# A graph layer on one core: gathering two groups ahead from group 44, and a paired group's permutation behind the gather

## The chip, the core and the metric

The kernel runs on one core of a Trainium2 chip. A core has five engines with a queue of instructions each: PE (TensorE, matrix products), ACT (ScalarE), DVE (VectorE), POOL (GpSimd) and SP (SyncE, which only issues DMAs here). Each engine works through its own queue in order and waits where an instruction needs another engine's result. The metric is device time in microseconds (us).

## The reference

A message-passing layer over 12,500 nodes with 128 features and 400,000 edges, sorted by `dst`:

```python
h = relu(layernorm(x)) @ W_in2f.T
Wij = (smu(edge_attr_20 @ W_f1.T + b_f1) @ W_f2.T + b_f2) * edge_weight[:, None]
agg = segment_sum(h[dst] * Wij, src, 12500)
out = x + smu(agg @ W_o1.T + b_o1) @ W_o2.T + b_o2
```

`smu(x)` is a smooth bend of `x`, made with erf. What is gathered is `h[dst]`, and the sum goes by `src`, which is in no order.

## The kernel before

**Tiles and groups.** The 400,000 edges are 3125 tiles of 128. Four tiles are a group (782 groups), two groups a super. The loop `for p in range(len(seq))` handles one group per turn; `at(p)` is the group of turn `p`. The supers are cut into ten epochs (`PARTS`, 56 supers or 112 groups each at first). The words "first pass" below mean the first epoch, turns 0 to 111.

**What happens to a group.** Its way is spread over several turns of the loop:

- `load` (SP): edge attributes `f`, targets `rbc` and the window `hw` of 42 rows of `h`, for the super three ahead;
- `pick_part` (ACT, two activations, lines 578 and 579): the 0/1 matrix `oh` that picks a row of the window for each edge;
- `hide` (PE, line 779) and `bend` (ACT, line 787): the hidden layer of the edge network, through the PSUM bank `pu`;
- `bins`, `count`, `read`, `number` (DVE and PE): for each edge the bin of 128 source nodes that it belongs to, and its place `ix` in that bin's buffer in DRAM;
- `gather` (PE, line 815): the product of `oh` and `hw` into the bank `ph`, which is `h[dst]`;
- `take` (ACT, line 834, four per group): that product times the edge weight, copied to `hg`;
- `weigh` (PE, lines 859 and 860): the edge network's output into the bank `pw`;
- `mix` (DVE, line 889): `pw` times `hg` into the rows `ms`, with the place inside the bin in column 128 (ACT);
- `send`, `scatter` (POOL, line 959): one indirect DMA per tile writes the 128 rows to their places.

**The sums.** In an epoch the rows that the epoch before wrote are read back (`fetch`, `rw`), a 0/1 matrix `se` is made (`choose`, DVE line 1004), and PE adds up the rows of each bin (`add`, line 1017) into a bank `pg`; after four bins DVE adds the bank to `agg` (line 1030). `parts` issues these products in two portions per turn. Where `pu_names` has two names, `pg` is always the bank `pg0`, and `parts` returns early rather than begin a new block of four bins with few products to go.

**Paired groups.** 125 groups are paired: their four tiles go out with two wide scatters and one extra one, `lt`, which a later group, the host, sends. `spread_keys`, `match` (DVE), `rank_left` and `place_left` make three pairs of 0/1 matrices, `permute` (PE, line 746, twelve products) brings the second two tiles' rows (`cd`) into the order of the first two, into the bank `pt`. `take_pairs` then reads that bank: DVE makes `lat`, the left-over rows' bin and place (lines 756 and 757), and ACT copies the rows (lines 759 and 760). `bins` and `number` of the host use `lat`, four or more groups later. Accesses of two engines to one bank are kept apart in the order in which the program issues them, reads too.

**The node stage.** During the first pass `step()` issues, three times a turn, the next of the steps that normalise `x`, transpose it, multiply it with the input weights, split it into three parts and write it to `h_dram`, through the banks `pg0` and `pg1` in turn; the splitting of the edge attributes stands there too (`todo`).

**Order.** The queues of PE, DVE, ACT and SP follow the order in which the program issues. What the turn does about the change, before:

```python
if p <= AHEAD_FROM:
    gather(at(p + 1)); take(at(p + 1))
parts(lo + (hi - lo) // 2)
mix(at(p + 1))
if g in paired:
    permute(g); take_pairs(g); send(g)
if at(p + 1) in paired:
    match(at(p + 1))
if p >= AHEAD_FROM:
    gather(at(p + 2)); take(at(p + 2))
```

(two calls to a line here). Behind it stand `hide` and `bend` for `p + 2`, or past `AHEAD_FROM` for `p + 3`, then `count(at(p + 2))`, `pick_part(at(p + 3))`, `bins(at(p + 3))`, `read(at(p + 2))`. `AHEAD_FROM` is 112, the first turn of the second pass; at that turn `pu_names` becomes `["pg1", "pu"]`, so that `hide` has two banks from there on.

Of the kernel before, what the change touches and what calls it, by code (L numbers as in the profile page):

```python
# [15 lines left out]
ALU = mybir.AluOpType  # L16
# [22 lines left out]
ROW = P + 1  # L39
# [3 lines left out]
NOBIN = 200.0  # L43
NOBIN_ROW = float(1 << 17)
# [3 lines left out]
def gnn_kernel(  # L48
# [19 lines left out]
    nc = tc.nc  # L68
# [14 lines left out]
    PER = SUP // GRP  # L83
    NG = (NT + GRP - 1) // GRP
    eps_of, left = [], NS
# [9 lines left out]
    for a, n in eps_of:  # L95
        paired = n if len(CAP) < len(eps_of) - SENT_LAST else 0
# [100 lines left out]
    drow = const.tile([P, EPOCHS], F32, name="drow")  # L197
# [124 lines left out]
    with tc.tile_pool(name="ld", bufs=4) as ld, \  # L322
# [24 lines left out]
        pu_names = ["pu"]  # L347
# [151 lines left out]
        def at(p):  # L499
            return seq[p] if p < len(seq) else NG  # L500
# [4 lines left out]
        epoch = [k for k, (a, n) in enumerate(eps_of) for _ in range(n)]  # L505
        first = {a * PER: k for k, (a, n) in enumerate(eps_of)}
        loaded, onehot, bins_of, slots, hidden, taken = {}, {}, {}, {}, {}, {}
        paired, host, wanting, since_pair = {}, {}, [], 0
# [75 lines left out]
        def s_of(g):  # L584
            return g // PER
# [143 lines left out]
        def place_left(g):  # L729
# [5 lines left out]
                                    irow_ps.unsqueeze(1).to_broadcast([P, 2, P]),  # L735
                                    at_.unsqueeze(2).to_broadcast([P, 2, P]), op=ALU.is_equal)

        def permute(g):

            pp, cd = matched.pop(g)[1], apart_of.pop(g)  # L740
            po = ps1.tile([P, GRP * P], F32, name="pt")
            for j in range(3):
                w = ROW + 2 if j == 2 else ROW
                for i in range(2):
                    o = (4 + i if j == 2 else 2 * i + j) * P
                    nc.tensor.matmul(po[:, j * (ROW + 2):j * (ROW + 2) + w], pp[:, o:o + P], cd[:, i, :w],  # L746
                                     start=(i == 0), stop=(i == 1))
            matched[g] = po

        def take_pairs(g):  # L750

            po, ms, k = matched.pop(g), mixed[g], epoch[s_of(g)]
            lt = cnt.tile([P, ROW], F32, name="lt", bufs=2)
            at_ = cnt.tile([P, 2], F32, name="lat")
            o = 2 * (ROW + 2)
            nc.vector.tensor_scalar(at_[:, 0:1], po[:, o + ROW:o + ROW + 1], NOBIN, None, op0=ALU.add)
            nc.vector.tensor_scalar(at_[:, 1:2], po[:, o + ROW + 1:o + ROW + 2], NOBIN_ROW, drow[:, k:k + 1],  # L757
                                    op0=ALU.add, op1=ALU.min)
            nc.scalar.activation(ms[:, 1::2, :], po[:, :o].rearrange("p (j r) -> p j r", j=2)[:, :, 0:ROW], AF.Copy)  # L759
            nc.scalar.activation(lt, po[:, o:o + ROW], AF.Copy)  # L760
            left_of[g] = (lt, at_[:, 0:1], at_[:, 1:2])
# [28 lines left out]
        def smooth(g):  # L790
            if g >= NG:
                return
            if new(g):
                units_of.pop(g)
                return
            n = groups[g][1] * P
            sm = edge.tile([P, GRP * P], F32, name="sm", bufs=3)
            nc.vector.scalar_tensor_tensor(sm[:, :n], units_of.pop(g)[:, :n], LIN, hidden[g][:, :n],
                                           op0=ALU.mult, op1=ALU.add)
            hidden[g] = sm  # L800
# [116 lines left out]
        def send(g):  # L917

            if by_edge(g):
                scatter(g, mixed.pop(g))  # L920
                return
            t, n = groups[g]
            ms = msg.tile([P, GRP, ROW], F32, name="ms")
            places_in(g, ms)
            pt = mixed.pop(g)
            for j in range(n):
                nc.scalar.activation(ms[:, j, 0:P], pt[:, j], AF.Copy, scale=w_sb[:, t + j:t + j + 1])
            if s_of(g) >= EARLY:
                nc.scalar.dma_start(kept_rows[:, t - kept_tile:t - kept_tile + n, :], ms[:, :n, :])
                return  # L930
            scatter(g, ms)
# [543 lines left out]
            todo.setdefault(10 + i, []).append(f)  # L1475

        k = 0
        SOON, SLACK, AHEAD_FROM = 10, 40, eps_of[1][0] * PER
        for p in range(len(seq)):
            g = seq[p]  # L1480
            s = g // PER
            if p == (FEW // SUP - 3) * PER:
                assert not opening
            if p % PER == 0:
                load(sup_at(p // PER + 3))
            if s < EARLY:
                k = chores(g)
            else:
                lo = hi = done
            if SOON < p < SLACK:  # L1490
                turn(at(p))
                send(at(p))
            if p >= SLACK:
                if by_edge(g) and g not in paired:
                    send(g)
                if p > SLACK and not by_edge(at(p - 1)):
                    turn(at(p - 1))
                    send(at(p - 1))
            for f in todo.pop(p, []):
                f()  # L1500
            if p > AHEAD_FROM:
                smooth(at(p + 2))
            step()
            number(at(p + 1))
            weigh(at(p + 1))
            if at(p + 1) in paired:
                spread_keys(at(p + 1))
            if p <= AHEAD_FROM:
                gather(at(p + 1))
                take(at(p + 1))  # L1510
            parts(lo + (hi - lo) // 2)
            mix(at(p + 1))
            if g in paired:
                permute(g)
                take_pairs(g)
                send(g)
            if at(p + 1) in paired:
                match(at(p + 1))
            if p >= AHEAD_FROM:
                gather(at(p + 2))  # L1520
                take(at(p + 2))
            if p == 0:
                turn(at(1))
                send(at(1))
            if p >= SOON:
                step()
            if p <= AHEAD_FROM:
                hide(at(p + 2))
                bend(at(p + 2))
            else:  # L1530
                hide(at(p + 3))
                bend(at(p + 3))
            if p < SOON:
                step()
            count(at(p + 2))
            if p <= AHEAD_FROM:
                smooth(at(p + 2))
            if 0 < p < SOON:
                turn(at(p + 1))
                send(at(p + 1))  # L1540
                if p == 1:
                    pick_part(at(3))
            if p == AHEAD_FROM:
                assert taken_steps == COUNT
                pu_names[:] = ["pg1", "pu"]
                hide(at(p + 3))
                bend(at(p + 3))
            pick_part(at(p + 3 - (p == 0)))
            bins(at(p + 3))
            if at(p + 1) in paired:  # L1550
                rank_left(at(p + 1))
            read(at(p + 2))
            if at(p + 1) in paired:
                place_left(at(p + 1))
            parts(hi)
            step()
            assert k == 0 or taken_steps == COUNT
# [291 lines left out]
```

## Time and profile before

| | us |
|---|---|
| median of three runs | 4024.81 (4022.95 to 4025.37) |
| profiled execution | 4014.04 |
| its span | 4012.3 |
| busy PE / DVE / ACT / POOL in the span | 3315.2 / 3264.7 / 2837.0 / 2949.5 |

The profile is one execution, told by the hardware profiler. Busy time counts an engine's instructions, not the DMAs that it issues nor the time it waits. A row of a group of instructions has the source line, the engine, the operation, what is written and read, the count, the busy time and the mean of one, and the idle time just before, with what ended it. A row of the list of waits has who waited, for whom, the total, the times and the longest. A row of the timeline has start, duration, engine, line, operation, operands, count and in brackets the idle time before.

### The profile page before, as it was taken

Reading aid. Unit: us, or ns where it says so; the run is one execution under the profiler, and the core shown is the slowest. Engines: PE = TensorE matmul, PEld = TensorE weight load, DVE = VectorE, ACT = ScalarE, POOL = GpSimd, SP = SyncE. Lnnn points to the kernel's source line nnn. Section 1 sums busy time; section 2 is a strip of 40 time slices with the busy share of each in tenths; the row PEclk is TensorE's granted clock in tenths of the full one; section 3 lists DMA queues with packets and bytes.
Section 4 is the critical chain, followed back from the end, with each engine's and each line's share of the span. In section 5 each row is a group of like instructions: output and inputs, shape, how many; then the busy total and the mean of one; then the engine's idle time right before and its main releaser. Section 6 shows DMA issues by size and latency. Waiting matters only on the chain.

```text
span 4012.3 us, 85549 instructions
## 1 busy us (share of the span) xinstructions
PE 3315.2 (83%) x25912; PEld 2821.8 (70%) x26245; DVE 3264.7 (81%) x8658; ACT 2837.0 (71%) x7473; POOL 2949.5 (74%) x3044
## 2 busy tenths in 40 slices
PE   7766776888888888888888888888988888798658
PEld 4345655777777777777777777777887777687548
DVE  7886667888888888888888888888998888897447
ACT  6757787777877777788788887777777777675002
POOL 6765657777777777777777777777777777777776
PEclk9878788999999999999999999999999999999889
DMA  5775767888987777887787778877888777786878
GB/s 165 228 220 165 210 185 232 256 254 248 267 248 227 225 211 216 229 240 214 211 230 229 220 230 235 231 220 225 237 238 235 210 204 221 211 244 203 269 239 252
DMA packets 659903, 906.21 MB, mean 226 GB/s; under 512 B 181396, under 2 KB 446488, under 8 KB 659306
## 3 DMA queue, kind: packets, MB, share of 16 engines
q1 hardware_dynamic: 552009, 673.07, 59.1%
q0 software_dynamic: 100112, 215.31, 16.6%
q10 hardware_dynamic: 7312, 12.29, 0.9%
q8 instruction: 208, 3.41, 0.4%
q14 instruction: 262, 2.14, 0.2%
HBM read 507.13 MB, written 393.21 MB: 224 GB/s over the span
## 4 chain that ended last, share of the span: by engine, by line
PE 24%; DVE 16%; DMA 16%; ACT 11%; issue 9%; POOL 8%; SPq 1%; DVEq 0%; ACTq 0%; POOLq 0%
DMA buf<-ms,ix 12%; PE pg L1017 8%; POOL buf L959 8%; PE pw L859 6%; DVE so L614 4%; ACT hg L834 4%; DVE ms L889 3%; PE pt L746 2%; DVE se L1004 2%; ACT oh L578 2%; DVE sl L671 2%; ACT ge L787 2%; PE ph L815 2%; ACT oh L579 1%; DVE mt L714 1%
## 5 line engine op out<-in xcount | busy, mean ns | idle before, releaser
L959 POOL DMA_INDIRECT buf<-ms,ix x2694 | 2611.9, 970 | 944.3 <-issue 653.0
L1017 PE MATMUL pg<-se,rw 128*128 128x128 f32 x8232 | 1230.8, 290 | 118.1 <-DVE se L1004 66.2
L1017 PEld LDWEIGHTS pg<-se,rw 128*128 128x128 f32 x8232 | 1065.0, 198 | 190.2 <-issue 95.3
L859 PE MATMUL pw<-w_f,ge 128*128 128x128 f32 x5568 | 1025.8, 307 | 109.1 <-DVE ms L889 79.1
L834 ACT ACTIVATE hg<-ph,w_sb 128x128 f32<-128x128 f32 x2784 | 790.3, 368 | 331.4 <-PE ph L815 317.2
L859 PEld LDWEIGHTS pw<-w_f,ge 128*128 128x128 f32 x5568 | 880.6, 199 | 169.4 <-ACT ge L787 67.3
L614 DVE SCALAR_TENSOR_TENSOR so<-irow_ps,hi_f,so 128x98 f16<-128x98 f32 x2693 | 855.3, 318 | 73.9
L1004 DVE TENSOR_TENSOR se<-irow_ps,rw 128x1536 f32<-128x1536 f32 (+1 forms) x353 | 602.3, 1706 | 150.9 <-DMA rw<-buf 112.6
L860 PE MATMUL pw<-wls,f 128*128 128x128 bf16 x2784 | 625.4, 225 | 0.0
L579 ACT ACTIVATE oh<-oh,onesb 128x512 bf16<-128x512 bf16 x780 | 562.6, 721 | 25.4
L578 ACT ACTIVATE oh<-rbc,nrow 128x512 bf16<-128x512 uint8 x762 | 566.9, 744 | 2.4 <-DMA rbc<-rel_dram 2.4
L889 DVE TENSOR_TENSOR ms<-pw,hg 128x512 f32<-128x512 f32 x571 | 392.2, 687 | 202.2 <-ACT hg L834 81.4
L671 DVE TENSOR_REDUCE sl<-pc 128x4 f32<-128x392 f32 (+1 forms) x782 | 448.5, 573 | 11.8 <-PE pc L644 7.0
L815 PE MATMUL ph<-hw,oh 126*128 126x128 bf16 x2784 | 281.7, 225 | 105.7 <-ACT oh L579 100.3
L815 PEld LDWEIGHTS <-oh 126*128 126x128 bf16 x2784 | 198.7, 100 | 166.5 <-ACT oh L579 154.0
L787 ACT ACTIVATE ge<-pu 128x512 f32<-128x512 f32 x447 | 273.2, 611 | 22.0 <-PE pu L779 16.8
L860 PEld LDWEIGHTS <-f 128*128 128x128 bf16 x2784 | 286.9, 103 | 0.0
L759 ACT ACTIVATE ms<-pt 128x258 f32<-128x258 f32 x125 | 48.3, 386 | 312.5 <-DVE lat L757 283.8
L641 PE MATMUL pc<-so,tri 128*128 128x392 f16 (+1 forms) x611 | 211.5, 346 | 21.5 <-DVE sl L671 4.8
L959 POOL DMA_INDIRECT buf<-ms,ix_kept x181 | 176.0, 972 | 55.2 <-issue 53.7
L787 ACT ACTIVATE ge<-pg 128x512 f32<-128x512 f32 (+1 forms) x334 | 204.8, 613 | 0.0
L746 PE MATMUL pt<-cd,mt 128*128 128x129 f32 x1500 | 201.2, 286 | 0.9 <-DVE at L733 0.5
(315 smaller groups left out, 4292.3 us busy)
## 6 DMA issues: line engine op xcount, KB each, us to landing
rw<-buf SPq DMA_DIRECT2D x300, 774.0 KB
f<-f_parts SPq DMA_DIRECT2D x370, 240.0 KB
buf<-zero SPq DMA_DIRECT2D x146, 387.0 KB
rbc<-rel_dram SPq DMA_DIRECT2D x389, 128.0 KB
buf<-ms,ix POOLq DMA_INDIRECT x2694
f_parts<-hs SPq DMA_DIRECT2D x106, 360.0 KB
rw<-buf SPq DMA_DIRECT2D x49, 645.0 KB
f_parts<-hs SPq DMA_DIRECT2D x108, 240.0 KB
```

Source lines behind the costliest of these rows:

```text
L578: nc.scalar.activation(oh, loaded[s][1][:, o:o + n], AF.Abs, bias=pneg if s < FEW // SUP else nrow)
L579: nc.scalar.activation(oh, oh, AF.Relu, scale=-1.0, bias=onesb[:, 0:1])
L614: nc.vector.scalar_tensor_tensor(so[:, j], irow_ps[:, :NB], hi_f[:, t + j:t + j + 1], since, op0=ALU.is_equal, op1=ALU.add)
L671: nc.vector.tensor_reduce(sl[:, :n], pc[:, :n], op=ALU.max, axis=AX.X)
L787: nc.scalar.activation(ge[:, :n], units_of[g][:, :n], AF.Gelu, scale=ZS)
L815: nc.tensor.matmul(ph[:, j * P:(j + 1) * P], oh[:3 * WIN, a:a + P], hw[:3 * WIN, g % PER, :], start=True, stop=True)
L834: nc.scalar.activation(hg[:, j * P:(j + 1) * P], rows_of[g][:, j * P:(j + 1) * P], AF.Copy, scale=w_sb[:, t + j:t + j + 1])
L859: nc.tensor.matmul(pw[:, a:a + P], ge[:, a:a + P], w_f2, start=True, stop=False)
L860: nc.tensor.matmul(pw[:, a:a + P], fb[:, o + a:o + a + P], wls, start=False, stop=True)
L959: i = nc.gpsimd.indirect_dma_start(out=(wide if g in host or g in paired else bufs)[k][:, :], out_offset=bass.IndirectOffsetOnAxis(ap=ix, ...
L1004: nc.vector.tensor_tensor(se[:, a:a + n], own.unsqueeze(1).to_broadcast([P, n, P]), rows_in[c][:, a:a + n, P:P + 1].to_broadcast([P, n, P] ...
L1017: nc.tensor.matmul(pgs[0][:, g, :], rows_in[c][:, o, 0:P], sel[c][:, o, :], start=(q == 0), stop=(q == Q[k] - 1))
```

## The change

- `AHEAD_FROM` is 44 instead of 112: from turn 44 on `gather` and `take` are issued two groups ahead and `hide` and `bend` three.
- In a paired group's turn `permute`, `take_pairs` and `send` stand behind `gather` and `take` of `p + 2` instead of ahead of them.
- `take_pairs` no longer makes `lat`; a new function `number_left` does, on DVE, after `pick_part` and ahead of `bins`.
- `pu_names` is no longer changed, as the node stage still uses `pg0` and `pg1` at turn 44: `hide` has the one bank `pu` throughout, and the sums alternate between `pg0` and `pg1`; the early return in `parts` no longer applies.
- `smooth` past `AHEAD_FROM` goes; for groups from 40 on it issues nothing.

```diff
+        left_at = {}
+        def number_left(g):
+            (po, at_), k = left_at.pop(g), epoch[s_of(g)]
+            nc.vector.tensor_scalar(at_[:, 0:1], po[:, 0:1], NOBIN, None, op0=ALU.add)
+            nc.vector.tensor_scalar(at_[:, 1:2], po[:, 1:2], NOBIN_ROW, drow[:, k:k + 1], op0=ALU.add, op1=ALU.min)
...
-            nc.vector.tensor_scalar(at_[:, 0:1], po[:, o + ROW:o + ROW + 1], NOBIN, None, op0=ALU.add)
-            nc.vector.tensor_scalar(at_[:, 1:2], po[:, o + ROW + 1:o + ROW + 2], NOBIN_ROW, drow[:, k:k + 1],
-                                    op0=ALU.add, op1=ALU.min)
+            left_at[g] = (po[:, o + ROW:o + ROW + 2], at_)
...
-        SOON, SLACK, AHEAD_FROM = 10, 40, eps_of[1][0] * PER
+        SOON, SLACK, AHEAD_FROM = 10, 40, 44
...
-            if p > AHEAD_FROM:
-                smooth(at(p + 2))
...
             mix(at(p + 1))
-            if g in paired:
-                permute(g)
-                take_pairs(g)
-                send(g)
             if at(p + 1) in paired:
                 match(at(p + 1))
             if p >= AHEAD_FROM:
                 gather(at(p + 2))
                 take(at(p + 2))
+            if g in paired:
+                permute(g)
+                take_pairs(g)
+                send(g)
...
             if p == AHEAD_FROM:
-                assert taken_steps == COUNT
-                pu_names[:] = ["pg1", "pu"]
                 hide(at(p + 3))
                 bend(at(p + 3))
             pick_part(at(p + 3 - (p == 0)))
+            if g in paired:
+                number_left(g)
             bins(at(p + 3))
```

## The prediction

> **What bounds the kernel now.** I read the page first, then busy time by stage, then the lists of waits, then single stretches of the timeline. The page:
>
> ```profile
> span 4012.3 us, 85549 instructions
> POOL 6765657777777777777777777777777777777776
> PEclk9878788999999999999999999999999999999889
> L959 POOL DMA_INDIRECT buf<-ms,ix x2694 | 2611.9, 970 | 944.3 <-issue 653.0
> ```
>
> POOL looks only seven tenths busy, yet its line is flat. Of each scatter the row shows 970 ns of work and, in 944.3 / 2694, 350 ns of idle time, most of it put down to "issue". So the flat sevens may be a full queue. Busy time by stage tells (columns: stretch, its length, then busy time and count for PE, PEld, DVE, ACT, POOL; then granted clock, DMA share, GB/s):
>
> ```profile
> 266.00:607.00 341.00, 242.96 (x1513) 194.39 (x1530) 221.32 (x709) 260.11 (x678) 203.69 (x211) 0.79 0.63 190
> 607.00:661.00 54.00, 34.86 (x259) 28.09 (x261) 35.30 (x107) 39.74 (x108) 41.19 (x43) 0.90 0.69 201
> 661.00:1216.00 555.00, 469.30 (x3818) 403.92 (x3873) 469.88 (x1281) 424.90 (x1154) 418.08 (x431) 0.97 0.87 256
> 1216.00:1760.00 544.00, 471.45 (x3888) 407.93 (x3940) 472.82 (x1283) 424.72 (x1153) 409.89 (x423) 0.98 0.77 223
> 1760.00:2302.00 542.00, 471.46 (x3891) 408.76 (x3946) 473.00 (x1289) 435.70 (x1150) 411.53 (x426) 0.98 0.76 222
> 2302.00:2763.00 461.00, 405.03 (x3397) 356.42 (x3442) 404.28 (x1068) 358.98 (x945) 341.86 (x352) 0.99 0.79 230
> 2763.00:3456.00 693.00, 593.21 (x5001) 530.02 (x5070) 591.66 (x1561) 504.75 (x1331) 526.58 (x546) 0.97 0.77 223
> 3456.00:3700.00 244.00, 185.25 (x193) 0.98 0.75 220
> 266.00:607.00 341.00, 31.67 (x55) 0.79 0.63 190
> 1216.00:1760.00 544.00, 71.48 (x125) 0.98 0.77 223
> ```
>
> The third row from the end is POOL's scatters alone: 193 in 244 us, one per 1.264 us, whatever group they belong to. That is the floor. Against it, scatters x 1.264 us and what is left of the stretch: 2763 to 3456, 690 of 693; 661 to 2763 (431 + 423 + 426 + 352 = 1632 scatters), 2063 of 2102, 39 us lost; 607 to 661, 54 of 54; 266 to 607, 267 of 341, **74 us lost**. So from 607 us POOL's scatters set the time, and only before that something else does. The last two rows count the per-group reduction of line 671, one per group: 341 / 55 = 6.20 us a group in the first pass, 544 / 125 = 4.35 in the third. The stretch 266 to 607 is groups 45 to 100, which the new constant 44 moves to the other order.
>
> Who waits in that stretch:
>
> ```profile
> ACT hg L834 <- PE ph L815: 58.4, 34, 6.0
> DVE ms L889 <- ACT hg L834: 56.1, 25, 6.4
> PEld pw L859 <- ACT ge L787: 38.8, 28, 2.8
> PE pw L859 <- DVE ms L889: 17.2, 11, 2.5
> ```
>
> It is a ring: PE's `gather`, ACT's `take`, DVE's `mix`, PE's next `weigh`; and ACT's `bend`, behind `take`, into the same `weigh`. At the end of the pass, with no step of the node stage in the way, the ring runs bare:
>
> ```profile
> 623.24 0.46 PE L859 MATMUL pw<-w_f,ge 128*128 128x128 f32 x2 [1.50 <-DVE ms L889]
> 624.59 0.39 PE L815 MATMUL ph<-hw,oh 126*128 126x128 bf16 x4
> 625.01 1.14 ACT L834 ACTIVATE hg<-ph,w_sb 128x128 f32<-128x128 f32 x4 [0.18 <-PE ph L815]
> 626.19 0.69 DVE L889 TENSOR_TENSOR ms<-pw,hg 128x512 f32<-128x512 f32 x1 [1.14 <-ACT hg L834]
> 627.02 0.46 PE L859 MATMUL pw<-w_f,ge 128*128 128x128 f32 x2 [1.50 <-DVE ms L889]
> ```
>
> From 623.24 to 627.02: 3.78 us a group. Of the 6.20 us, some 2.4 are thus the node stage's steps, splits and paired groups, each of which lengthens the ring it stands in.
>
> **The change part by part.** *Two groups ahead from 44.* `mix(p+1)` finds its `take` done an iteration earlier, and `weigh(p+2)` its `bend`. The ring shrinks to `weigh` and `mix`, 1.35 + 0.69 us. Nothing is added: each group has the same matmuls, copies and DMAs, on the same queues. What is next in line? ACT has 260.11 / 55 = 4.73 us of work a group in this stretch, PE 4.42, POOL 211 x 1.264 / 55 = 4.85. ACT still waits in each iteration for `gather`, which itself waits for ACT's `oh`. Ends: at best POOL's 4.85, a gain of 55 x 1.35 = 74 us; at worst the steps hold PE and ACT in step as before, 0. The largest ACT share I know here is
>
> ```profile
> 340.00:400.00 60.00, 42.38 (x294) 34.22 (x294) 39.27 (x116) 51.43 (x136) 38.04 (x39) 0.86 0.65 191
> ```
>
> 51.43 / 60 = 0.857, still in the old order; at that share 4.73 us become 5.52, a gain of 37. I take 0.89, between that and the 0.975 that POOL would allow and nearer to the row: 5.3 us a group, 55 x 0.90 = **49 us**. Groups 101 to 112 gain nothing, POOL being full there. `hide` and `bend` are issued twice at 44 and no longer at 112: 0.
>
> SP: the loads of a pair of groups stay in their iteration, while `gather` comes one group earlier, so of the four or five groups of lead one is used up, about 5 us. SP's longest wait there is
>
> ```profile
> SPq L272 <- DVE ix L693: 19.0, 5, 13.1
> ```
>
> 13.1 us, inside the three or four groups (16 us and more) that remain. Ends 0 and one such wait, 13 us; I take 0, as SP's other waits are shorter.
>
> *One bank for `pu`, two for `pg`.* From 112 on the old kernel gave `hide` two banks; the new one has one, and `hide(p+3)` must wait until `bend(p+2)` has read it. The queues cover that:
>
> ```profile
> 2007.28 0.63 ACT L787 ACTIVATE ge<-pg 128x512 f32<-128x512 f32 x1
> 2008.55 0.72 ACT L579 ACTIVATE oh<-oh,onesb 128x512 bf16<-128x512 bf16 x1
> 2009.33 0.40 PE L815 MATMUL ph<-hw,oh 126*128 126x128 bf16 x4 [0.39 <-ACT oh L579]
> 2009.56 0.38 PE L779 MATMUL pu<-f,w1s 128*128 128x512 bf16 x1
> ```
>
> `gather` stands before `hide` on PE and waits for `oh`, which ACT makes after `bend`. When PE reaches `hide`, the bank has been read for 1.65 us (2007.91 to 2009.56). Cost 0, by order. In return the sums of four bins alternate between two banks and PE no longer waits for the addition on DVE, 46.2 us in all, and the early return in `parts` never fires; PE isn't the bound there, so 0 to a few us.
>
> [...]
>
> *The paired group.* Before:
>
> ```profile
> 2003.91 1.51 PE L746 MATMUL pt<-cd,mt 128*128 128x129 f32 x12
> 2004.72 0.68 DVE L889 TENSOR_TENSOR ms<-pw,hg 128x512 f32<-128x512 f32 x1
> 2005.26 0.39 PE L815 MATMUL ph<-hw,oh 126*128 126x128 bf16 x4
> 2005.54 0.21 DVE L757 TENSOR_SCALAR lat<-pt,drow 128x1 f32<-128x1 f32 x1
> 2005.84 0.39 ACT L759 ACTIVATE ms<-pt 128x258 f32<-128x258 f32 x1 [1.47 <-DVE lat L757]
> 2006.12 0.27 ACT L760 ACTIVATE lt<-pt 128x129 f32<-128x129 f32 x1
> 2006.28 1.15 ACT L834 ACTIVATE hg<-ph,w_sb 128x128 f32<-128x128 f32 x4
> ACT ms L759 <- DVE lat L757: 283.8, 111, 8.0
> DVE lat L756 <- PE pt L746: 74.7, 68, 4.9
> PE pg L1017 <- DVE agg L1030: 46.2, 56, 4.9
> 661.00:2763.00 2102.00, 16.70 (x80) 0.98 0.80 233
> ```
>
> ACT stands 283.8 / 111 = 2.6 us behind the permutation and `lat`, with `take`, `bend` and `pick_part` queued behind it. In the new order, on these durations: `gather` 2003.91 to 2004.3, permutation to 2005.8, `take` 2004.4 to 2005.55 beside it, line 759 at 2005.85, line 760 done at 2006.4, then `lat` on DVE until 2006.8. ACT is through all three 1.0 us earlier (2007.43 before); DVE's `lat`, and the four bin comparisons and the reduction queued behind it, are 1.05 us later (2005.75 before). POOL gets its rows at the same moment. What does 1.05 us on DVE cost? Bounds: nothing if DVE would idle anyway, 1.05 x 80 = 84 us if DVE carried each of the 80 paired groups between 661 and 2763 (the last row above counts line 757; after 2763 POOL is 3 us short of full, and hides it). DVE is busy 472.82 of 544, so it has 0.57 us of idle time in a plain group, and in a paired one also PE's 1.5 us of permutation, which lengthens the group but not DVE's work; I take it as covered. The freed ACT time eases `gather`; from the 39 us that POOL loses between 661 and 2763 I take back 6, ends -39 and +84.
>
> **Sum.** -49 - 6 = -55 us, no change after 2763. The profiled execution took 4014.04 us for its span of 4012.3, and would be at 3959; the median of the runs, 4024.81, lies 10.8 above it, so 3970.
>
> **The rivals.** *The pass follows POOL at once* (3936): PE's clock was granted at 0.79 in this stretch and 0.97 to 0.99 later; if PE's gaps close, its 4.42 us shrink to 4.42 x 0.79 / 0.97 = 3.6 and the steps cost less. Then all 74 us go, and 15 of the 39: 4025 - 89. Against it: ACT's 4.73 us don't shrink with that clock. [...]
>
> *The steps bind, not the order* (4018): the node stage's chain of normalise, transpose, cut and product runs PE, ACT, PE, ACT by itself, and ACT remains in lockstep through `oh`. The order gains a tenth of the 74 us. For it: 2.4 of 6.20 us come from there. Against it: those waits are on the ring now, and the group of slack takes them off.
>
> *`lat` becomes the wait* (4060): ACT's copies are late, DVE stands before the bin comparisons, and POOL's numbers come late. It decides once DVE's extra wait passes the idle time of a paired group, about 1 us. Fully exposed: 4025 - 49 + 84. Against it: POOL, full to 98% over these stretches, must first run out of work before a late number costs anything.
>
> *`pu`'s single bank binds* (4146): if `hide` met `bend`, each of the 125 groups of a pass would hold PE up to 0.63 us; PE's idle time there, (544 - 471.45) / 125 = 0.58 us a group, consists of other waits already; if half of it moved under this one, 0.34 us stay, and over the some 500 groups before 2763 that is 170 us: 4025 - 49 + 170. Against it: the order of the two queues above. [...]
>
> **How the numbers follow.** Forecast (gains 25 to 74) 0.60, at once 0.07, steps bind 0.16 (0.06 of it within 0.2%, about 8 us, which is what a measurement can tell), `lat` 0.12, single bank 0.05. Faster 0.60 + 0.07 + 0.10 = 0.77, same 0.06, slower 0.17. The range leaves out the far part of the first rival and the slower half of the last two: 3938 to 4028. The forecast's own range is 3945 to 4000.
>
> **What will show it.** 266 us onwards: 211 scatters in about 290 us instead of 341, ACT near 0.89, the wait of line 834 for line 815 down, `mix` no longer waiting for `hg`. The list of waits has no line 759 behind `lat`, but `lat` behind line 760. POOL from 661 on as before. Wrong would be: 6 us a group again in the first pass, a wait of line 779 for line 787, or fewer than 78 scatters per 100 us after it.

## The result, and the profile after

The changed kernel took 4005.97 us (median of five runs, 4001.16 to 4019.24) against 4025.37 us for the kernel before beside it (five runs, 4022.95 to 4030.57). The ratio is 0.9954, with a 95% interval of 0.9939 to 0.997: faster by 18.5 us as the ratio has it, and by more than the 0.2% that a measurement can tell. The same kernel was measured twice more below, at 0.9942 and 0.993. The forecast of 3970 us has the sign right and less than half of its gain came: 18.5 of 55 us here, 23 of 55 as the mean of the three measurements.

One thing is needed to read some of the runs further down: nine of them fell on chips on which the kernel before itself takes 5900 to 5960 us instead of 4020, and each is compared only with the kernel before on its own chip.

The page of the kernel after, its span, POOL's busy tenths in 40 slices, and the two groups that the change touches most:

```profile
span 4017.5 us, 85745 instructions
POOL 6766667777777777777777777677777777777776
...
L965 POOL DMA_INDIRECT buf<-ms,ix x2694 | 2612.1, 970 | 950.2 <-issue 598.2
...
L785 PE MATMUL pu<-f,w1s 128*128 128x512 bf16 x742 | 292.3, 394 | 8.5 <-DMA f<-f_parts 7.9
```

This profiled execution took 4019.24 us, the slowest of its five; its span is even 5 us longer than that of the profiled execution of before. Line 785 is `hide`, which used to be line 779: this group waits 8.5 us in the whole run, nearly all of it for a DMA. Over all of line 785 a single wait, of 0.6 us, stands against `bend` (line 793), which empties the one bank `pu`.

Busy time by stage (stretch, length, then busy time and count for PE, PEld, DVE, ACT, POOL; granted clock, DMA share, GB/s):

```profile
266.00:607.00 341.00, 251.70 (x1698) 197.06 (x1696) 243.62 (x770) 285.61 (x746) 228.60 (x235) 0.84 0.72 207
...
661.00:1216.00 555.00, 467.46 (x3794) 403.37 (x3795) 457.78 (x1238) 408.01 (x1098) 401.50 (x416) 0.95 0.87 248
...
2763.00:3456.00 693.00, 597.80 (x5079) 535.02 (x5078) 591.02 (x1561) 507.30 (x1327) 526.99 (x545) 0.97 0.80 224
```

In 266 to 607 us POOL began 235 scatters where it was 211. At the floor of 1.264 us each, the 24 more are 30 us. ACT went from 260.11 to 285.61 us busy, a share of 0.84 and not 0.89. From 661 to 1216 us there are 416 scatters instead of 431: 15 fewer, 19 us given back.

That gives a way of keeping accounts for the profiles on ordinary chips. In all forms of the scatter line every kernel issues 3000 scatters (2694 of them in the row above), so a lead of n scatters at some point is worth n x 1.264 us if POOL stays full behind it. Counts of that line, in 0 to 661 us and in 661 to 3700 us; the last two columns are the difference of both counts from before, times 1.264 us, and the span less that of before, 4012.3 us:

| kernel | to 661 | 661 to 3700 | by the counts | span |
|---|---|---|---|---|
| before | 436 | 2367 | 0 | 0 |
| after | 461 | 2337 | +6 | +5 |
| whole change, first repeat | 465 | 2349 | -14 | -16 |
| whole change, second repeat | 463 | 2354 | -18 | -20 |
| two groups ahead alone | 460 | 2357 | -18 | -19 |
| paired group's order alone | 450 | 2355 | -3 | -3 |
| one bank alone | 440 | 2357 | +8 | +8 |

The counts give the span to within some 2 us in these seven and within 3 us in the four profiles not listed. This is bookkeeping: what has been scattered by 3700 us need not be scattered afterwards. It tells when time was won or lost, and not by what. By 661 us every kernel of this study with the order two groups ahead has a lead of 22 to 31 scatters on an ordinary chip. What is lost later differs from one execution to the next: the kernel with only the banks changed, whose median is that of before, shows 10 fewer from 661 to 3700 us in its profiled execution. The profile of before is one of its good ones (4014.04 us against a median of 4024.81), that of after one of its bad ones.

Where the first pass gained is told by ACT's idle time. Groups of ACT's instructions between 266 and 607 us (busy, mean ns, then idle time before and what ended it), before:

```profile
L834 ACT ACTIVATE hg<-ph,w_sb 128x128 f32<-128x128 f32 x220 | 62.3, 366 | 58.5 <-PE ph L815 58.4
...
L759 ACT ACTIVATE ms<-pt 128x258 f32<-128x258 f32 x10 | 3.9, 386 | 15.7 <-DVE lat L757 12.5 <-PE pu L779 1.8 <-PE pg L249 1.4
```

And after, for the same 55 turns, which now take 267.7 to 578 us:

```profile
L840 ACT ACTIVATE hg<-ph,w_sb 128x128 f32<-128x128 f32 x220 | 62.1, 364 | 31.4 <-PE ph L821 31.2
...
L264 ACT ACTIVATE hs<-pg 128x512 bf16<-128x512 f32 (+1 forms) x24 | 13.9, 582 | 6.9 <-DMA h_dram<-hs 6.9
...
L765 ACT ACTIVATE ms<-pt 128x258 f32<-128x258 f32 x10 | 3.9, 393 | 4.0 <-PE pt L754 4.0
```

Busy time of all engines (columns as above) in five turns at the end of the node stage, nearly bare of its steps, and in these 55 turns:

```profile
582.00:599.50 17.50, 11.64 (x103) 9.12 (x102) 14.09 (x39) 16.06 (x43) 13.48 (x14) 1.00 0.65 180
267.70:578.00 310.30, 230.53 (x1538) 180.39 (x1537) 221.49 (x710) 260.12 (x680) 205.72 (x212) 0.83 0.71 208
```

ACT does the same 260.12 us of work for these 55 groups, in 310.3 us instead of 341. So its idle time fell from 80.9 to 50.2 us, by 30.7: 27.1 of it ahead of `take`, 11.7 ahead of the paired groups' copies, less 6.9 for a new wait of the node stage for a DMA (line 264) and 1.3 at line 243. `take` still waits 31.4 us, 31.2 of it for `gather`. From the list of waits in 266 to 607 us (who waited, for whom, total, times, longest):

```profile
PEld L821 <- ACT oh L579: 35.5, 30, 5.2
ACT hg L840 <- PE ph L821: 33.9, 23, 4.8
PE ph L821 <- ACT oh L579: 27.3, 26, 4.9
PEld pw L865 <- DVE ms L895: 25.2, 19, 3.5
```

`mix` waiting for `take` (56.1 us before) and `weigh` waiting for `bend` (38.8) are gone from the list. The rows look like a ring of two in their place: `gather` waits for ACT's `oh`, and ACT's next `take` waits for `gather`. At the end of the node stage that ring does run (timeline of ACT: start, duration, line, operation, idle time before):

```profile
587.42 1.14 ACT L840 ACTIVATE hg<-ph,w_sb 128x128 f32<-128x128 f32 x4 [0.39 <-PE ph L821]
...
589.69 0.72 ACT L579 ACTIVATE oh<-oh,onesb 128x512 bf16<-128x512 bf16 x1
...
590.90 0.88 ACT L840 ACTIVATE hg<-ph,w_sb 128x128 f32<-128x128 f32 x3 [0.39 <-PE ph L821]
```

3.48 us from one `take` to the next, in which ACT idles 0.39 us; in 582 to 599.5 us it is busy 16.06 of 17.5. Before, the bare ring took 3.78 us.

In the 55 turns it isn't what ACT waits for. Taken one by one in the timeline, the 31.2 us are 19 waits of `take`, and in 18 of them `oh` had been done for 0.2 to 4.9 us when `gather` began: PE was late for another reason. The one that stands behind `oh` is 0.39 us. Two of the others, from the timelines of PE and ACT:

```profile
277.19 0.80 PE L865 MATMUL pw<-w_f,ge 128*128 128x128 f32 x2 [3.27 <-DVE ms L895]
...
280.48 1.14 ACT L840 ACTIVATE hg<-ph,w_sb 128x128 f32<-128x128 f32 x4 [4.18 <-PE ph L821]
...
325.32 0.72 ACT L579 ACTIVATE oh<-oh,onesb 128x512 bf16<-128x512 bf16 x1
326.58 2.08 PE L257 MATMUL pg<-w_in,rw 128*128 128x128 f32 x8 [0.26 <-ACT rw L252]
330.90 0.45 PE L821 MATMUL ph<-hw,oh 126*128 126x128 bf16 x4
331.38 1.14 ACT L840 ACTIVATE hg<-ph,w_sb 128x128 f32<-128x128 f32 x4 [4.76 <-PE ph L821]
```

In the first, `weigh`, which stands ahead of `gather` in PE's queue, had waited for DVE's `mix`, which came behind the node stage's statistics on DVE. In the second, `oh` is done at 326.04 and `gather` begins at 330.90, behind eight products of the node stage and `weigh`. By PE's last wait ahead of `gather`, the 31.2 us split into 8.8 behind `mix` (4 waits), 7.2 behind DVE's keys for the paired groups' `match` (line 705, 4), 10.8 behind ACT in the node stage's transposes and products (lines 249 and 257, 3), 0.4 behind `oh` (1), and 4.1 where PE was still at `weigh`'s products (7). Most of the large waits stand at the corresponding places in the two repeats of this kernel too, and in the kernel with two groups ahead alone.

### The profile page after: what moved, and what is told of

Read it like the earlier page. It is cut to its first block, busy times and chain, and to the rows that moved or that the text cites. A ratio compares the mean times of both kernels' runs of the same rounds, so it can differ in the third digit from the quotient of the medians.

```text
span 4017.5 us, 85745 instructions
## 1 busy us (share of the span) xinstructions
PE 3335.0 (83%) x26245; PEld 2832.7 (71%) x26245; DVE 3262.0 (81%) x8658; ACT 2850.9 (71%) x7473; POOL 2947.3 (73%) x3044
## 4 chain that ended last, share of the span: by engine, by line
PE 26%; DMA 19%; DVE 18%; issue 9%; POOL 8%; ACT 6%; SPq 1%; DVEq 0%; ACTq 0%; POOLq 0%
DMA buf<-ms,ix 15%; PE pg L1023 9%; POOL buf L965 8%; PE pw L865 6%; DVE so L614 5%; DVE se L1010 3%; PE pt L754 3%; DVE ms L895 3%; DVE sl L671 2%; ACT hg L840 2%; PE ph L821 2%; DMA f<-f_parts 1%; PE pw L866 1%; DVE mt L714 1%; ACT oh L578 1%
## 5 line engine op out<-in xcount | busy, mean ns | idle before, releaser
L840 ACT ACTIVATE hg<-ph,w_sb 128x128 f32<-128x128 f32 x2784 | 790.2, 366 | 537.9 <-PE ph L821 513.7
L865 PE MATMUL pw<-w_f,ge 128*128 128x128 f32 x5568 | 1040.1, 310 | 150.9 <-DVE ms L895 145.0
L793 ACT ACTIVATE ge<-pu 128x512 f32<-128x512 f32 x781 | 475.4, 609 | 28.3 <-PE pu L785 25.5
L821 PEld LDWEIGHTS <-oh 126*128 126x128 bf16 x2784 | 208.0, 101 | 135.1 <-ACT oh L579 118.6
L785 PE MATMUL pu<-f,w1s 128*128 128x512 bf16 x742 | 292.3, 394 | 8.5 <-DMA f<-f_parts 7.9
L643 PE MATMUL pc<-so,rest_h 128*128 128x294 f16 (+1 forms) x611 | 186.3, 305 | 0.0
```

Source lines behind the costliest of these rows:

```text
L821: nc.tensor.matmul(ph[:, j * P:(j + 1) * P], oh[:3 * WIN, a:a + P], hw[:3 * WIN, g % PER, :], start=True, stop=True)
L840: nc.scalar.activation(hg[:, j * P:(j + 1) * P], rows_of[g][:, j * P:(j + 1) * P], AF.Copy, scale=w_sb[:, t + j:t + j + 1])
L865: nc.tensor.matmul(pw[:, a:a + P], ge[:, a:a + P], w_f2, start=True, stop=False)
```

## The experiments

**The parts alone.** From the kernel before, `AHEAD_FROM = 44` and nothing else (`hide` gets its second bank at turn 112 as before, a paired group stands where it stood, `lat` is made inside `take_pairs`):

```diff
-        SOON, SLACK, AHEAD_FROM = 10, 40, eps_of[1][0] * PER
+        SOON, SLACK, AHEAD_FROM = 10, 40, 44
...
-            if p > AHEAD_FROM:
-                smooth(at(p + 2))
...
             if p == AHEAD_FROM:
-                assert taken_steps == COUNT
-                pu_names[:] = ["pg1", "pu"]
                 hide(at(p + 3))
                 bend(at(p + 3))
+            if p == eps_of[1][0] * PER:
+                assert taken_steps == COUNT
+                pu_names[:] = ["pg1", "pu"]
```

> The other order from group 44 alone: the paired group's turn and lat stand as before, and from 112 on the hidden layer has two banks as before. Theory (the paired group's new order costs time in the passes after the first): the first pass gives 30 to 45 us and nothing takes it back, about 3985. Rival one (the single bank costs): also about 3985. Rival two (the first pass gives only what the whole change gave): about 4006.

From the kernel before, the banks alone: one bank `pu`, the sums alternating, no early return:

```diff
             if p == AHEAD_FROM:
-                assert taken_steps == COUNT
-                pu_names[:] = ["pg1", "pu"]
```

> The kernel before with one change: pu keeps one bank after 112, and the sums alternate between pg0 and pg1. Theory: 0 to 3 us either way, about 4025. Rival one (the single bank costs the 20 us or so that the first pass won beyond the result): about 4045. Rival two: 4025.

From the kernel before, the paired group alone: `permute`, `take_pairs` and `send` behind `gather` and `take`, `lat` made by `number_left` ahead of `bins`:

```diff
             mix(at(p + 1))
-            if g in paired:
-                permute(g)
-                take_pairs(g)
-                send(g)
...
                 take(at(p + 2))
+            if g in paired:
+                permute(g)
+                take_pairs(g)
+                send(g)
...
+            if g in paired:
+                number_left(g)
             bins(at(p + 3))
```

> The kernel before with one change: the paired group's permutation, copies and send behind gather and take, and lat behind pick_part. Theory: the 80 paired groups between 661 and 2763 each lengthen by some 1 us, of which 15 to 30 us reach the end: 4040 to 4055. Rivals one and two: 4025.

And the first two together, the whole change without the paired group's order:

> The whole change without the paired group's new order: from 44 two groups ahead, one bank for pu, two for the sums. Theory: about 3985, as e1_ahead. Rival one: about 4006, the single bank being in it. Rival two: 4006.

Measured, against 4020.03 us (23 runs) on the same chip:

| | us (runs) | ratio | 95% |
|---|---|---|---|
| two groups ahead | 3987.19 (6) | 0.9924 | 0.991 to 0.9938 |
| banks | 4022.5 (12) | 1.001 | 0.9996 to 1.0023 |
| paired group | 4018.11 (12) | 0.9999 | 0.9987 to 1.0011 |
| two groups ahead and banks | 3996.86 (6) | 0.9956 | 0.9939 to 0.9973 |

The gain is that of the order two groups ahead. The 4040 to 4055 us expected of the paired group's order alone and the 4045 us of the rival for the single bank did not come; 3996.86 lies between what was expected of the two together. Busy time by stage for the scatter line alone (stretch, length, busy and count, clock, DMA share, GB/s), first with two groups ahead alone, then with the paired group alone, then with the banks alone:

```profile
266.00:607.00 341.00, 224.95 (x232) 0.84 0.69 206
661.00:2763.00 2102.00, 1576.04 (x1623) 0.97 0.80 231
```

```profile
266.00:607.00 341.00, 213.51 (x220) 0.83 0.66 195
661.00:2763.00 2102.00, 1570.66 (x1618) 0.98 0.80 231
```

```profile
266.00:607.00 341.00, 204.25 (x211) 0.78 0.64 191
661.00:2763.00 2102.00, 1571.19 (x1621) 0.98 0.80 232
```

211 scatters became 232 by the order, 220 by the paired group, 211 by the banks. ACT's idle time in that stretch splits in the same way (58.5 ahead of `take` and 15.7 ahead of the copies before); with two groups ahead alone:

```profile
L841 ACT ACTIVATE hg<-ph,w_sb 128x128 f32<-128x128 f32 x250 | 70.8, 367 | 29.2 <-PE ph L822 28.9
...
L766 ACT ACTIVATE ms<-pt 128x258 f32<-128x258 f32 x10 | 3.9, 386 | 21.8 <-DVE lat L744 21.8
```

and with the paired group alone:

```profile
L840 ACT ACTIVATE hg<-ph,w_sb 128x128 f32<-128x128 f32 x235 | 66.8, 366 | 57.9 <-PE ph L821 57.7
...
L765 ACT ACTIVATE ms<-pt 128x258 f32<-128x258 f32 x10 | 3.9, 387 | 6.2 <-PE pt L754 6.2
```

The first halves the wait of `take` and does not lower that of the copies; the second does the opposite. Nine scatters are worth 11 us in the first pass, but the paired group alone is not faster by the end, so it gives them back. Over the whole run its waits are (first fence), where before they were (second)

```profile
ACT hg L840 <- PE ph L821: 571.5, 507, 6.0
DVE lat L743 <- ACT lt L766: 160.3, 112, 5.9
```

```profile
ACT hg L834 <- PE ph L815: 317.2, 369, 6.0
```

and the copies waited 283.8 us for `lat` besides. That wait is gone; the one of `take` grew by 254 us, and DVE waits 160.3 us for ACT's copies, where it waited 74.7 us for the permutation. The wait has moved. Worked out from the starts of line 671, the turn in which the permutation falls takes some 0.8 us longer than before in the later passes (6.06 against 5.23 us, 80 of the turns 112 to 586) and each of the other 394 some 0.13 us less (4.14 against 4.27). That is 66 us more and 52 less, 15 us more in all, which is about what was won before.

With the banks alone, PE waits less for DVE's addition to `agg`, as forecast, and the ratio is 1.001. Its row in the list of waits of the whole run:

```profile
PE pg L1024 <- DVE agg L1037: 11.1, 5, 5.9
```

That is 35 us less than before. Taking the second bank from `hide` and giving it to the sums made no difference that the runs can tell. That POOL, not PE, set the time there is the reading of the counts, and no run here tests it.

**Does the single bank cost anything under the new order?** The two kernels with two groups ahead differ by 10 us, with and without the banks, so that a cost of some 12 us for the single bank was open. Three kernels and a repeat on one chip: one bank `pu` with the sums on `pg0` alone and the early return kept; one bank with the sums alternating and the early return kept (both with the paired group in its old place); the whole change with the second bank for `hide` from turn 112 on; the whole change again.

```diff
-                pgs[0] = bank("pg") if pu_names == ["pu"] else ps1.tile([P, GRP, P], F32, name="pg0")
+                pgs[0] = bank("pg") if not past_first[0] else ps1.tile([P, GRP, P], F32, name="pg0")
...
-                full = len(pu_names) > 1 and b % GRP == 0 and q == 0
+                full = past_first[0] and b % GRP == 0 and q == 0
```

(`past_first[0]` becomes true at turn 112; the second kernel has only the second of these two edits. The third has the switch of `pu_names` at turn 112, as in the first experiment.)

> e1_ahead with one bank for pu all along; the sums keep to pg0 and the early return of parts stays, so pg1 lies unused after the first pass. Theory (the single bank of pu is what separates e1_ahead, ratio 0.9924, from e4_ahead_banks, 0.9956): 0.995 to 0.996. Rival (the single bank is free by the order of ACT's queue, as predicted, and the sums' new placing is what costs): 0.992.

> e4_ahead_banks with the early return of parts kept: one bank for pu, the sums alternate between pg0 and pg1. Theory (single bank of pu): 0.9955, as e4_ahead_banks. Rival (without the early return the first portion of the sums runs on into a new block and holds up gather and permute): 0.992 to 0.993.

> The whole change, but from 112 on pu has two banks and the sums pg0, as in the kernel before. Theory (banks cost some 12 us in the whole change, the paired group's order nothing): 0.992, as e1_ahead. Rival (the paired group's order takes back what it gives once the passes after the first run closer to POOL): 0.995.

> The whole change again, beside the others on one chip: 0.9954 as before, that is about 18 us faster than before, by all theories.

Measured, against 4019.13 us (11 runs):

| | us (runs) | ratio | 95% | scatters 266 to 607 |
|---|---|---|---|---|
| one `pu`, sums on one bank | 3994.15 (5) | 0.9939 | 0.9926 to 0.9952 | 231 |
| one `pu`, sums alternate, early return | 3995.21 (5) | 0.9942 | 0.9929 to 0.9954 | 231 |
| whole change, two banks for `hide` | 3997.23 (6) | 0.9949 | 0.9937 to 0.9961 | 238 |
| whole change again | 3996.52 (6) | 0.9942 | 0.993 to 0.9954 | 237 |

All four are the same within their intervals. Giving the second bank back to the whole change gains nothing, and the first two lie between what the theory and its rival expected; a cost of the single bank is not found, though one of a few us is not excluded. The kernel of the first experiment was not measured again here; the 10 us between it and the fourth show in none of these kernels, so that 3987.19 us is no proof of a better version. The paired group's order brings six or seven scatters in the first pass here too, and no time, as the rival of the third expected.

**What holds the first pass now?** Four kernels on the whole change. Two copies of 128x128 more on ACT in turns 45 to 99; the node stage's transposes and products left out beyond the first 512 rows; two of `weigh`'s products issued twice; three additions of 128x128 more on DVE:

```diff
+            if 45 <= p < 100:
+                nc.scalar.activation(more, zero[:, 0:P], AF.Copy)
+                nc.scalar.activation(more, zero[:, P:2 * P], AF.Copy)
```

> The whole change with two copies of 128x128 more on ACT at the end of each of the turns 45 to 99, some 0.55 us or 30 us in all. Theory (in the first pass PE and ACT run in lockstep through the node stage's steps, and no single engine's work is the bound): a half to all of it shows in the first pass, 385 to 400 us from turn 44 to 112 instead of 367 to 370. Rival (ACT's own work is the bound, as the prediction had it): all 30 us, 400. Rival two (POOL): under 8 us.

```diff
         def turned():
+            if b >= HEAD:
+                return
...
         def cut():
-            nc.scalar.activation(xt[:, :n], kept[0][:, :n], AF.Relu)
+            nc.scalar.activation(xt[:, :n], xn[:, :n] if b >= HEAD else kept[0][:, :n], AF.Relu)
...
         def product():
+            if b >= HEAD:
+                kept[0] = xt
+                return
```

> The whole change with the node stage's transposes and products left out for the rows beyond the first 512 (their h is not the reference's): ACT and DVE do all their steps, from SBUF instead of PSUM, and PE has no part in them. Theory (the round trips of the node stage between ACT and PE cost about half of the 2.4 us that its steps add to a turn): the first pass falls from about 368 to 330 to 345 us. Rival (ACT's work is the bound): 360 to 368, as ACT's work stays.

```diff
+                if 46 <= place_of[g // PER] * PER + g % PER < 101 and a < 2 * P:
+                    nc.tensor.matmul(pw[:, a:a + P], ge[:, a:a + P], w_f2, start=True, stop=True)
```

> The whole change with two products of weigh issued twice in turns 45 to 99, 0.4 to 0.8 us of PE a turn, 24 to 45 us in all. Theory (lockstep of PE and ACT): a half to all of it shows, the first pass takes 385 to 405 us. Rival (ACT's work is the bound): under 10 us.

```diff
+            if 45 <= p < 100:
+                for i in range(3):
+                    nc.vector.tensor_add(more, zero[:, i * P:(i + 1) * P], zero[:, i * P:(i + 1) * P])
```

> The whole change with three additions of 128x128 more on DVE at the end of each of the turns 45 to 99, some 0.5 us or 28 us in all. Theory (lockstep of PE and ACT, DVE beside it): under a third of it, 368 to 378 us for the first pass. A rival in which DVE stands in the ring as well: 390 or more.

They fell on a chip where the kernel before takes 5935.47 us. The same four on a second chip, which was of the same kind, 5904.7 us for the kernel before:

> As h1_act_more, beside a kernel before of about 4020 us. Theory (lockstep of PE and ACT): 385 to 400 us from turn 44 to 112 instead of 367 to 370. Rival (ACT's own work is the bound): 400. Rival two (POOL): under 376.

> As h2_no_node_pe (the node stage's transposes and products left out beyond the first 512 rows, their h is not the reference's). Theory (round trips of the steps): 330 to 345 us from turn 44 to 112. Rival (ACT's work): 360 to 368.

> As h3_pe_more. Theory (lockstep): 385 to 405 us from turn 44 to 112. Rival (ACT's work): under 378.

> As h4_dve_more. Theory (DVE stands beside the lockstep): 368 to 378 us from turn 44 to 112. A rival in which DVE stands in the ring as well: 390 or more.

The one that leaves work out a third time, and the whole change; these two fell on different chips, 5960.35 and 4023.81 us for the kernel before:

> As h2_no_node_pe, hoped for beside a kernel before of about 4020 us (the node stage's transposes and products left out beyond the first 512 rows; their h is not the reference's). Theory (round trips of the node stage's steps between ACT and PE): 330 to 345 us from turn 44 to 112 instead of 365 to 372. Rival (ACT's own work): 360 to 368.

> The whole change. On a chip where the kernel before takes about 5900 us, with i1 to i4 at 486, 464, 491 and 491 us from turn 44 to 112: theory (lockstep of PE and ACT) 465 to 475, so that additions on PE and ACT show by more than half and the node stage's products take off under 10 us there; rival (ACT's work) 456 to 460, so that ACT's copies show in full and the others do too by chance. On a chip of about 4020 us: 365 to 372 and a ratio near 0.995, as before.

| | first chip | second | third | scatters 266 to 607 |
|---|---|---|---|---|
| ACT more | 1.0073 (1.0042 to 1.0104) | 1.0037 (1.0013 to 1.0062) | | 181, 178 |
| node products out | 1.006 (1.004 to 1.008) | 0.9977 (0.9951 to 1.0003) | 1.0034 (1.0016 to 1.0053) | 187, 190, 183 |
| PE more | 1.0092 (1.0063 to 1.012) | 1.0029 (1.0004 to 1.0054) | | 177, 177 |
| DVE more | 1.0102 (1.0078 to 1.0126) | 1.0026 (1.0001 to 1.005) | | 174, 177 |

The whole change on the ordinary chip: 3994.15 us (5 runs), ratio 0.993 (0.9916 to 0.9944), 236 scatters in 266 to 607 us; turns 44 to 112 took 368 us by the starts of line 671, as expected.

As an experiment the question stays open. The times expected for the first pass were for an ordinary chip, where the same order begins 231 to 238 scatters in the stretch; on these chips it is 174 to 181 with work added and 183 to 190 with the node stage's products left out. The ratios of one kernel differ by up to 0.008 between the chips, more than the kernels on one chip differ among themselves, and the whole change without an edit was not measured there, so that neither figure can be set against it. What these runs allow is only this: on such chips an addition on ACT isn't dearer than one on PE or DVE, which speaks against ACT alone as the bound there. For the ordinary chip the reading rests on the waits listed one by one above, and no run has taken their causes away.

## Why the prediction was right and wrong

**The floor: right as a price, and not reached everywhere.** One scatter per 1.264 us of POOL, whatever the group, is what a lead of the first pass is worth: in the six profiles set against that of before, the counts give the span to within some 2 us. But "from 607 us POOL's scatters set the time" is only nearly so. At the floor 661 to 2763 us would hold 2102 / 1.264 = 1663 scatters; before has 1630 there, and the kernels with the change have fewer, so a lead can be lost there again.

**Two groups ahead, 49 us: the gain right, its size and what limits it wrong.** The step that failed is "at that share 4.73 us become 5.52 ... I take 0.89 ... 5.3 us a group", and under it the overlap that was to allow that share: "those waits are on the ring now, and the group of slack takes them off". The rows of line 671, after, the first and the last of the 55 turns that the prediction counted, and then five turns at the end of the node stage:

```profile
267.73 0.56 DVE L671 TENSOR_REDUCE sl<-pc 128x4 f32<-128x392 f32 x1
...
577.95 0.56 DVE L671 TENSOR_REDUCE sl<-pc 128x4 f32<-128x392 f32 x1
...
582.08 0.56 DVE L671 TENSOR_REDUCE sl<-pc 128x4 f32<-128x392 f32 x1
...
599.26 0.56 DVE L671 TENSOR_REDUCE sl<-pc 128x4 f32<-128x392 f32 x1
```

310.2 / 55 = 5.64 us a group, ACT 260.12 of 310.3 busy, a share of 0.84. The saving is 0.56 us a group, 31 us with the paired groups' part of it and some 26 us (21 scatters) without, where 0.90 and 49 were forecast. The ring did go: `mix` and `weigh` no longer wait for ACT. But the steps' waits did not go with it. Of the 50.2 us that ACT still idles, 31.2 stand behind `gather`, 26.8 of them where PE itself had waited for `mix`, for the paired groups' `match` or in the node stage; `gather` comes behind these in PE's queue in the new order as in the old. Five of these waits stand at corresponding places in both profiles, behind lines 249, 257 and 705: 12.9 us before, 9.0 after. The slack takes off the waits for `take` and `bend`, and not these. The prediction's other sentence on ACT, that it "still waits in each iteration for `gather`, which itself waits for ACT's `oh`", doesn't fit either: ACT waits in 19 of 55 turns, and in one of them behind `oh`. What the time would be without the steps, no run on an ordinary chip shows.

**The rival "the steps bind, not the order" (4018): half right.** The first half of its mechanism, the node stage's chain through PE and ACT, is part of what remains, with the paired groups' `match` and DVE's statistics beside it. The second half, lockstep through `oh`, is 0.39 us in these turns. Its price, a tenth of the 74 us, is not: the order got some 26 us. A turn near the end of the stage takes 17.18 / 5 = 3.44 us, so of the 5.64 us 2.20 still come from the steps and the paired groups, 2.41 before.

**The rival "at once" (3936): wrong**, for the reason given against it. The granted clock rose only from 0.79 to 0.84, and ACT's 260 us of work stayed what they were. PE's 3.6 us a group was an estimate, and no run shows it or that the clock rises as PE's gaps close: in the 55 turns PE has 230.53 / 55 = 4.19 us a group at 0.83, busy for 0.74 of the time, while the five turns at the end of the node stage were granted 1.00 with PE busy for 11.64 of 17.5 us, a share of 0.67.

**The single bank, 0: right.** One wait of line 785 for line 793 in the kernel after, of 0.6 us, ratio 1.001 for the banks alone (0.9996 to 1.0023), and no gain from giving the second bank back. The sums' 46.2 us of waits went and brought nothing, within the "0 to a few us". From 2763 to 3456 us 545 scatters stand against 546, as forecast. SP's longest wait for `ix` in the first pass is 10.0 us (13.1 before), so its 0 holds too:

```profile
SPq L272 <- DVE ix L693: 11.2, 4, 10.0
```

**The paired group, -6 us: the schedule right, the gain not there.** The timeline after, and then two rows of the list of waits of its whole run:

```profile
2013.27 0.40 PE L821 MATMUL ph<-hw,oh 126*128 126x128 bf16 x4
...
2013.50 1.56 PE L754 MATMUL pt<-cd,mt 128*128 128x129 f32 x12
...
2013.83 1.12 ACT L840 ACTIVATE hg<-ph,w_sb 128x128 f32<-128x128 f32 x4
...
2015.10 0.39 ACT L765 ACTIVATE ms<-pt 128x258 f32<-128x258 f32 x1 [0.16 <-PE pt L754]
...
2015.38 0.27 ACT L766 ACTIVATE lt<-pt 128x129 f32<-128x129 f32 x1
...
2015.69 0.16 DVE L743 TENSOR_SCALAR lat<-pt 128x1 f32<-128x1 f32 x1
2015.76 0.21 DVE L744 TENSOR_SCALAR lat<-pt,drow 128x1 f32<-128x1 f32 x1
```

```profile
ACT hg L840 <- PE ph L821: 513.7, 466, 11.4
DVE lat L743 <- ACT lt L766: 158.1, 101, 3.3
```

Counted from `gather`, the copies begin after 1.83 us (1.94 forecast) and `lat` is done after 2.70 (2.89). Of ACT's 2.6 us of waiting per paired group 0.3 are left, as the step says (37.7 us in 116 waits for line 754), but `take` now waits 513.7 us for `gather`, 317.2 before, and `lat` 158.1 us for ACT. In these rows the reads of `pt` by the two engines come one after the other: ACT's second copy ends at 2015.38 + 0.27 = 2015.65, DVE's first read begins at 2015.69. In the first pass the step alone was worth 9 scatters, 11 us, which the forecast did not have. Between 661 and 2763 us the four kernels with two groups ahead and this step have 1600, 1615, 1618 and 1626 scatters, the four with two groups ahead and without it 1621 to 1627; so there is no saving of 6 us, and more likely a loss. The rival "`lat` becomes the wait" has its wait, and not its price of 84 us.

**The sum.** By 661 us the three profiles of the whole change lead by 25 to 29 scatters, 32 to 37 us; at the end 18.5 to 28 us are left by the ratios. So of the 55 us forecast, about 20 were never won in the first pass, and part of what was won was lost again. The counts place that between 661 and 2763 us, 1600 to 1618 scatters where the forecast had 1630 and some five more; leads and counts are of one profile each, the ratios of five or six runs.

**The markers.** "Fewer than 78 scatters per 100 us" was badly set: before had 1630 / 21.02 = 77.5 itself. The others spoke plainly, ACT's 0.84 and 235 scatters where the forecast needed 211 in 290 us, which is 248 in 341.

## What to carry to other kernels

Before an order is credited with removing waits, go through the large ones of the stage singly in the timeline and ask what each stands behind; here a group of slack reached those on the ring that it opened, and not those of other work ahead in the same queue (26.8 of the 31.2 us that `take` still waits). A row in the list of waits names the engine that released last, not what held that engine up: here "ACT behind `gather`" and "`gather` behind `oh`" stood one above the other and were, but for one wait in 19, not the same turns. Count a queue that may be full by items per time, since the line of POOL, which began a scatter per 1.264 us, shows seven tenths, and keep accounts in its items; a wait that only moves between two other engines brought none here (283.8 us of ACT behind `lat` gone, ratio 0.9999). Measure the parts of a change alone before any of them is blamed, and repeat a difference of 10 us in 4000 on another chip before it is believed.

## What was not expected of the hardware

The same kernel takes 4020 us on some chips and 5900 to 5960 us on others. For one of the latter (the kernel with more work on ACT, second chip, span 5924.5 us) ACT's first wait over the whole run, and busy time by stage of the scatter line:

```profile
ACT hg L841 <- remote: 1178.4, 212, 10.8
```

```profile
661.00:2763.00 2102.00, 1019.15 (x1057) 0.81 0.51 152
```

A place of that wait in its timeline:

```profile
2488.86 0.39 PE L822 MATMUL ph<-hw,oh 126*128 126x128 bf16 x4
...
2493.67 1.14 ACT L841 ACTIVATE hg<-ph,w_sb 128x128 f32<-128x128 f32 x4 [7.09 <-remote]
```

The instructions of ACT and POOL seen here take as long as in the kernel after: the four of `take` 1.14 us in both, a scatter 1019.15 / 1057 = 0.96 us against 1550.48 / 1600 = 0.97 in the same stretch. PE's mean over all its products there is longer, 1397.67 / 9433 = 0.148 us against 1819.94 / 14953 = 0.122 in the kernel after. And `take` starts 4.4 us after `gather` is done, on a release that the profile can't place on this core, 212 times with 1178.4 us in all; POOL begins 1057 scatters in 661 to 2763 us instead of 1600 to 1630. The clock granted to PE is 0.81 there against 0.97 in the kernel after. What differs between the chips isn't known from these runs, and the wait explains some 1180 of the 1900 us at most.
